# Image indices placed chunk by chunk, image 0's first strips between the chunks, and row sends one turn later, in a fused block-matching and convolution kernel

## The chip, the core and the metric

The kernel runs on one core of a Trainium2 chip. The metric is device time in microseconds (us), the median of several runs of the whole program. The engines are TensorE (PE, matmul; its weight loads are PEld), VectorE (DVE), ScalarE (ACT), GpSimd (POOL) and SyncE (SP). POOL and SP issue nearly all DMAs.

## What is computed

The input is eight images of 32 channels by 128 x 128 in float32. Layer 0 normalises an image in groups of two channels, then finds for each pixel the 8 offsets of a 5 x 5 window whose 3 x 3 patches are nearest, gathers the 8 shifted copies (256 channels), and runs three rounds of a 1 x 1 convolution (256 to 256) and a 3 x 3 depthwise convolution. A grouped 1 x 1 mix of the gathered copies (dct) is multiplied in, two more mixes bring it to 32 channels, and x is added. Layer 1 normalises again, applies one 5 x 5 kernel to each channel and adds.

```python
def _L0_conv_ref(x, dct_w, w1, w2, w3, w4, w5, w6, inv_dct_w, agg_w):
    ...
    xb = _patch_match_stack(x)
    dct = _conv(xb, dct_w, groups=C)
    h = jax.nn.relu(_conv(_conv(xb, w1), w2, groups=CK, pad=1))
    h = jax.nn.relu(_conv(_conv(h, w3), w4, groups=CK, pad=1))
    wiener = jax.nn.sigmoid(_conv(_conv(h, w5), w6, groups=CK, pad=1))
    filt = _conv(wiener * dct, inv_dct_w, groups=C)
    return _conv(filt, agg_w)
...
x = x + _L0_conv_ref(_gn(x), L0_conv_dct_w, L0_conv_w1, L0_conv_w2, L0_conv_w3, L0_conv_w4,
                     L0_conv_w5, L0_conv_w6, L0_conv_inv_dct_w, L0_conv_agg_w)
x = x + _L1_conv_ref(_gn(x), L1_conv_kernel, 1, 2)
```

## The kernel before

**Two streams of work.** The *convolution* of an image is cut into 16 steps of 8 rows, and a 17th step that finishes what lags (`steps`, pairs of image b and step n). The *preparation* of an image makes the offset indices that its gather needs. Image 0 is prepared alone at the start; image b+1 is prepared inside the steps of image b.

**Preparation** (`prep`, L338) works on four row groups of 32 rows, one on each 32 partitions. It loads the image `xn` (one buffer), normalises it, and takes six slices (i) of six rows. In a slice there are six pairs of differences `df` on DVE (L411), their squares on ACT (L419), sums over channels on PE into `pd` (L426), and a copy `sm` that goes to DRAM as `sq` (`squares`). After slices 1, 3, 4 and 5, `costs` is pushed for chunk 0, 1, 2 and 3: eight rows in each row group. It loads `dsum` back, sums the 3 x 3 patches (L475 to L487), turns the result with PE into `pt` and ACT's copy `ct`, and for each row takes four MAX8 and FIND_INDEX8 on DVE (`mx`, `idx`). A counter, `left`, pushes `places` when the last of the 32 rows of maxima is done. `places` (L511) turns offset indices into gather positions: for each of the four row groups, seven DVE operations on `o` and `cn`, two turns on PE (`pi`), two copies on ACT (`li`), two DMAs on POOL into the DRAM table `idxd`. When the four are issued the image is `ready`.

**Gather.** A strip is four rows; it is fetched in two units g. `gather_load` (POOL) loads pixels `xt` (three buffers) once a strip, and two broadcast index tiles `ib` (five buffers). `gather_select` (ACT, L585 and L586) turns them into `sel`, and `gather_pixels` (PE, L600, and a copy `xb` on ACT, L607) picks the pixels. Seven units are loaded and four gathered before the first step; in the loop, pixels run one step ahead and loads three units further.

**A step** of the convolution goes over i = 3, 2, 1, 0: depth i of the three convolutions, each one step behind the one before, and i = 0 for the end of a step (`final_dct`, `final_add`). Depth i has a half on DVE (`depthwise_v`: one ACT and eight DVE operations L689 on the tile `tv`, 10.5 us together) and a half on PE (`depthwise_t`: 48 matmuls `pw`, L709, on the tile `t`). After `pointwise_t`, SP shifts rows inside `t` (L671, L673); `pw` needs them. `rows_before_t` (L617) and `rows_before_v` (L624) send the last rows of `t` and `tv` to their top for the *next* step, on SP; at an image's end a POOL memset stands in for them (L619, L626).

**What sets the order.** PE, DVE and ACT run in program order; the order on POOL and SP is chosen when the program is built. Preparation tasks are generators that wait in four queues: D (DVE work, with a cost in us), A, P and Q (follow-up work on ACT and PE). `tick` is called once in each i and pays out D work: `total / (NS - 2)` us a step, so an image's preparation is spread over 14 steps. `until(cond, 4.0)` instead runs all queues in a loop until a condition holds, with no step in between. Before the first step it runs till image 0 is ready, and at step 15 till the next image is. `prep(b + 1)` is pushed at step 0 of image b.

The order inside one i, which both edits touch, is:

```python
next(new_v, None)            # 8 DVE taps of depth i
if live and i: pointwise_t(i, bi, ni, lws[i - 1], src)
if not i: next(dt, None)     # pw of the depth before
if s < len(steps): unit(gather_pixels, u)
...
if i: next(dt, None)         # pw of the depth before
run("A")
next(dv, None)               # activation, then rows_before_v
next(dt, None)               # activations, then rows_before_t
dv, dt = new_v, new_t
```

Of the kernel before, what the change touches and what calls it, by code (L numbers as in the profile page):

```python
# [43 lines left out]
def bm3d_conv_preact(  # L44
# [293 lines left out]
    def prep(b):  # L338

        xn = load_image(b, nc.gpsimd) if b else first  # L340
        yield "P", 0
        yield "D", 5.5
        st = work.tile([P, 8, 6], F32, name=f"st_{b}", tag="st")
        for i in range(8):
            nc.vector.bn_stats(
                st[:, i], xn[:, 3 + 4 * i : 7 + 4 * i, 2 : 2 + W]
            )
        mv = work.tile([P, 2], F32, name=f"mv_{b}", tag="mv")
        nc.vector.bn_aggr(mv, st.rearrange("p a b -> p (a b)"))
        yield "A", 0  # L350
        nc.scalar.copy(xn[:, :, 0:2], xn[:, :, 2:3].to_broadcast([P, HR, 2]))
        nc.scalar.copy(
            xn[:, :, 2 + W :], xn[:, :, 1 + W : 2 + W].to_broadcast([P, HR, 2])
        )
        mr = yield from group_stats(mv, f"a{b}")
        nc.vector.tensor_scalar(
            xn, xn, mr[:, 0:1], mr[:, 1:2], op0=ALU.subtract, op1=ALU.mult
        )
        push(sources(b, xn))

        idx = work.tile([P, 4, 8, K, 4], U32, name=f"idx_{b}", tag="idx", bufs=1)

        sq = dram.tile([NO // 2, 4, HR - 2, HX], F32, name=f"sq_{b}", tag="sq")
        left = [32]
        for i in range((HR - 2) // SR):
            pd = ps_d.tile([P, SR // 2, HX], F32, name=f"pd_{b}_{i}", tag="pd")

            for aa in ((2, 4), (0, 0), (1, 1), (3, 2), (4, 3), (5, 5)):
                yield "D", PAIR
                push(squares(b, i, pd, xn, aa, sq, idx, left))  # L370

    def sources(b, xn):

# [23 lines left out]
                xt[:, ja:jz, t], xl[:, at : at + 1].to_broadcast([H, jz - ja, C])  # L397
            )

    def squares(b, i, pd, xn, aa, sq, idx, left):  # L400


        r0 = SR * i
        ds = []
        for e in range(2):
            o = 13 + 2 * aa[e] + e
            dy, dx = o // 5 - 2, o % 5 - 2

            ca, cz = max(0, -dx), min(HX, HX - dx)
            df = work.tile([P, SR, HX], F32, name=f"df_{b}_{i}_{o}", tag="df", bufs=4)  # L410
            nc.vector.tensor_sub(  # L411
                df[:, :, ca:cz],
                xn[:, r0 : r0 + SR, ca:cz],
                xn[:, r0 + dy : r0 + dy + SR, ca + dx : cz + dx],
            )
            ds.append((df, ca, cz))
        yield "A", 0
        for df, ca, cz in ds:
            nc.scalar.activation(df[:, :, ca:cz], df[:, :, ca:cz], AF.Square)  # L419
        yield "Q", 0  # L420

        for e in range(2):
            for h in range(2):
                df, ca, cz = ds[e]
                j = 2 * e + h
                nc.tensor.matmul(  # L426
                    pd[C * j : C * (j + 1), :, ca:cz],
                    neg[:, 28 - 4 * aa[e] : 60 - 4 * aa[e]],
                    df[:, SR // 2 * h : SR // 2 * (h + 1), ca:cz],
                    start=aa[0] == 2,  # L430
                    stop=aa[0] == 5,
                    skip_group_check=True,
                )
        if aa[0] < 5:
            return
        sm = work.tile([P, SR // 2, HX], F32, name=f"sm_{b}_{i}", tag="sm", bufs=1)
        nc.scalar.copy(sm, pd)
        for e in range(2):
            for h in range(2):
                j = 2 * e + h  # L440
                nc.gpsimd.dma_start(
                    sq[e::2, :, r0 + SR // 2 * h : r0 + SR // 2 * (h + 1)].rearrange(
                        "o g r x -> o g (r x)"
                    ),
                    sm[C * j : C * j + 24].rearrange("p r x -> p (r x)"),
                )

        q = {1: 0, 3: 1, 4: 2, 5: 3}.get(i)
        if q is not None:
            push(costs(b, q, sq, idx, left))  # L450

    def costs(b, i, sq, idx, left):

        yield "A", 0, 2
        while held:
# [32 lines left out]
        for h in range(0, R, 4):  # L488
# [9 lines left out]
            for q in range(4):  # L498
                yield "D", 1.85
                y = 8 * i + h + q  # L500
                for rg in range(4):
                    c25 = ct[:, q, rg : rg + 4 * NO - 3 : 4]
                    nc.vector.max(mx[:, 4 * q + rg], c25)
                    nc.vector.max_index(
                        idx[:, rg, y // 4, :, y % 4], mx[:, 4 * q + rg], c25
                    )
                left[0] -= 1
                if not left[0]:
                    push(places(b, idx))

    def places(b, idx):  # L511

        dst = idxd[b] = dram.tile([32, K * 4, W], BF16, name=f"idxd_{b}", tag="idxd")
        for rg in range(4):
            yield "D", 2.6
            o = work.tile([P, 256], F32, name=f"o_{b}_{rg}", tag="lin_o", bufs=1)
            ct = work.tile([P, 256], F32, name=f"cn_{b}_{rg}", tag="lin_c", bufs=1)
            nc.vector.tensor_copy(o, idx[:, rg].rearrange("p s k y -> p (s k y)"))
            nc.vector.tensor_scalar(ct, o, 5.0, None, op0=ALU.is_ge)
            for lim in (10.0, 15.0, 20.0):  # L520
                nc.vector.scalar_tensor_tensor(
                    ct, o, lim, ct, op0=ALU.is_ge, op1=ALU.add
                )
            nc.vector.scalar_tensor_tensor(
                o, ct, float(QW - 5), o, op0=ALU.mult, op1=ALU.add
            )
            o3 = o.rearrange("p (s y) -> p s y", y=4)
            nc.vector.tensor_tensor(
                o3,
                o3,  # L530
                cst[:, C_BASE : C_BASE + 4].unsqueeze(1).to_broadcast([P, 64, 4]),
                ALU.add,
            )
            yield "P", 0
            for h in range(2):
                pt = ps_x.tile([P, 512], F32, name=f"pi_{b}_{rg}_{h}", tag="x")
                nc.tensor.transpose(pt[:, :P], o[:, h * P : (h + 1) * P], ident)
                li = work.tile([P, P], BF16, name=f"li_{b}_{rg}_{h}", tag="li")
                nc.scalar.copy(li, pt[:, :P])
                s = 8 * rg + 4 * h  # L540
                nc.gpsimd.dma_start(
                    dst[s : s + 4].rearrange("s k x -> (s k) x"), li
                )
        ready.add(b)

    ready = set()
    xbs, xts, ibs, selss = {}, {}, {}, {}
# [1 line left out]
    def gather_load(b, s4, g):  # L549
# [16 lines left out]
        for k2 in range(2):  # L566
            ib = work.tile(
                [P, 2, 4, W], BF16, name=f"ib_{b}_{s4}_{g}_{k2}", tag="ib", bufs=5
            )
            k0 = 4 * g + 2 * k2  # L570
            nc.gpsimd.dma_start(  # L571
                ib.rearrange("p k y x -> p (k y x)"),
                idxd[b][s4, 4 * k0 : 4 * k0 + 8]
                .rearrange("k x -> (k x)")
                .partition_broadcast(P),
            )
            ibs[b, s4, g, k2] = ib
# [97 lines left out]
    def depthwise_v(i, b, n):  # L675
# [15 lines left out]
                )  # L691
        yield
        nc.scalar.activation(acc, acc, funcs[i - 1])
        rows_before_v(i, b, n)

    def depthwise_t(i, b, n):
# [169 lines left out]

    def unit(stage, u):
        if 0 <= u < len(units) and units[u]:
            stage(*units[u])

    def source(i, b, n):
# [8 lines left out]
    total = 5.5 + 3.3 + 36 * 1.95 + 4 * 4.6 + 32 * 1.85 + 4 * 2.6 + 8 * 2.1  # L880
    owed = [0.0]

    def tick(i):

        now[0] += 1
        owed[0] += total / (NS - 2) * (0.4 if i == 0 else 0.2)
        owed[0] -= run("D", owed[0]) if owed[0] > 0 else 0
        owed[0] = min(owed[0], 6.0)

# [8 lines left out]
    with tc.manual_schedule(engines=ORDERED):  # L898
        push(prep(0))
        push(mixes())  # L900
        until(lambda: 0 in ready, 4.0)
        xbd[0] = dram.tile([P, 2, H, W], F32, name="xbd_0", tag="xbd")
        for i in range(3):
            nc.gpsimd.memset(tb[i][0:64, :, 0], 0.0)
# [3 lines left out]
            unit(gather_pixels, u - 3)  # L908
        u = 4

        dt = dv = iter(())

        later = lambda: None

        for s in range(len(steps) + 2):
            if s < len(steps):
                b, n = steps[s]
                if s == 2:
                    push(bands())
                if n == 0 and b + 1 < NB:  # L920
                    push(prep(b + 1))
                if n == NS - 1 and b + 1 < NB:
                    until(lambda: b + 1 in ready, 4.0)
# [1 line left out]
            for i in (3, 2, 1, 0):  # L925
# [23 lines left out]
                if s < len(steps):  # L949
                    unit(gather_select, u + 1)  # L950
                    unit(gather_load, u + 3)
                    tick(i)
                next(new_v, None)
                if live and i:
                    pointwise_t(i, bi, ni, lws[i - 1], src)
                if not i:
                    next(dt, None)
                if s < len(steps):
# [4 lines left out]
                run("A")  # L963
                next(dv, None)
                next(dt, None)
                dv, dt = new_v, new_t
                if live and not i:
                    later = partial(end, bi, ni, xr, j0, j1)
                if not i and 0 <= s - 1 < len(steps):
                    fins[s - 1] = final_load(*steps[s - 1])  # L970
        later()
        until(lambda: NB - 1 in done, 4.0)

# [61 lines left out]
```

## Time and profile before

| | us |
|---|---|
| Median of 3 runs | 7167.68 (7158.68 to 7188.37) |
| The profiled execution, its own time | 7169.27 |
| Its span, first to last instruction | 7167.5 |
| Mean granted TensorE clock | 0.977 |
| First `pg` (gather) / first `pv` of step 0 of image 0 | 214.4 / 241.6 |
| Step 0 of images 1 and 2 | 1070.0 / 1940.2 |
| Last matmul `pw` begins | 7086.6 |
| PE / DVE / ACT / POOL busy | 6709.5 / 5835.6 / 5061.9 / 2716.4 |

A line of the profile names the engine, the line of the kernel, the operation and the tiles as out<-in. A group's idle figure is the engine's idle time just ahead of its instructions, with what ended it. The slices cut the span in 40 pieces of 179 us; a digit is tenths. The page's chain of what ended last covers only the end of this run, from about 7000 us, so the start and the steps are read from the timeline and from busy times in stretches. Times in those are from the first instruction on.

### The profile page before, as it was taken

The page shows a single profiled execution, that of the slowest core. Times are in us where ns is not written, and L with a number is a line of the kernel's source. Part 1 is how long each engine was busy: PE and PEld are TensorE (multiplying, and loading weights), DVE is VectorE, ACT ScalarE, POOL GpSimd, SP SyncE. Part 2 cuts the span into 40 slices and gives each one's busy share as a digit, 9 for nine tenths or more (in the row PEclk, how much of TensorE's full clock was granted, in tenths as well). Part 3 has the DMA queues.
Part 4 walks back from the last instruction along what each step waited for, and adds up shares of the span by engine and source line. Part 5 has one row for each costly group of instructions (what it writes and reads, how often), then busy time and mean ns, then how long its engine had stood idle before and what let it go on. Part 6 is the DMA issues. An engine that isn't in the chain of part 4 may idle for free. (4 is left out here: it accounts for less than half of the span.)

```text
span 7167.5 us, 229467 instructions
## 1 busy us (share of the span) xinstructions
PE 6709.5 (94%) x100226; PEld 3178.5 (44%) x100226; DVE 5835.6 (81%) x8606; ACT 5061.9 (71%) x6704; POOL 2716.4 (38%) x4599
## 2 busy tenths in 40 slices
PE   4699999999999999999999999999999999999997
PEld 1344444444444444444444444444444444444443
DVE  7689878788788888888888888888888889767675
ACT  4777668677686777767677776877668677676662
POOL 6343335333353333533344333543335333232222
PEclk7799999999999999999999999999999999999999
DMA  3476656667566665756656565666656655556652
GB/s 82 120 163 146 149 136 152 139 148 152 131 157 143 141 152 125 165 147 138 151 125 160 141 149 134 144 156 147 148 134 143 161 137 148 129 148 140 143 136 63
DMA packets 762413, 1007.47 MB, mean 141 GB/s; under 512 B 211425, under 2 KB 575009, under 8 KB 761409
## 3 DMA queue, kind: packets, MB, share of 16 engines
q0 software_dynamic: 375328, 733.44, 42.2%
q1 hardware_dynamic: 381056, 256.86, 17.1%
q8 instruction: 788, 12.91, 0.8%
q10 hardware_dynamic: 5024, 2.49, 0.2%
q14 instruction: 217, 1.77, 0.1%
HBM read 542.24 MB, written 217.01 MB: 106 GB/s over the span
## 5 line engine op out<-in xcount | busy, mean ns | idle before, releaser
L689 DVE SCALAR_TENSOR_TENSOR acc<-tv,dwv,acc 128x1024 f32<-128x1024 f32 (+1 forms) x3264 | 4083.7, 1252 | 214.6 <-ACT acc L686 103.2
L709 PE MATMUL pw<-t,dwd 128*32 128x508 f32 (+6 forms) x19584 | 2174.5, 591 | 151.3 <-DMA t<-t 116.0
L709 PEld LDWEIGHTS pw<-t,dwd 128*32 128x32 f32 (+1 forms) x19584 | 702.9, 111 | 1384.1 <-issue 1182.2
L571 POOL DMA_DIRECT2D ib<-idxd x1024 | 570.9, 558 | 1803.4 <-ACT sel L586 1611.8
L585 ACT ACTIVATE ib<-ib,nplace 128x1024 bf16<-128x1024 bf16 x1024 | 1165.5, 1138 | 16.6 <-DMA ib<-idxd 16.6
L586 ACT ACTIVATE sel<-ib 128x1024 f32<-128x1024 bf16 x1024 | 1084.4, 1059 | 32.6
L661 PE MATMUL p<-acc,lw 128*32 128x256 f32 x17408 | 994.6, 375 | 20.2 <-issue 20.2
L638 PE MATMUL pv<-acc,lw 128*128 128x512 f32 (+1 forms) x2112 | 979.8, 607 | 8.0 <-DVE acc L760 3.9
L607 ACT COPY xb<-pg 128x512 f32<-128x512 f32 x512 | 303.9, 594 | 732.8 <-PE pg L600 732.6
L646 ACT COPY tv<-pv 128x512 f32<-128x512 f32 (+2 forms) x784 | 445.6, 584 | 493.6 <-PE pv L638 483.1
L661 PEld LDWEIGHTS p<-acc,lw 128*32 128x32 f32 x17408 | 565.2, 110 | 441.2 <-issue 99.6
L600 PEld LDWEIGHTS pg<-sel,xt 128*32 128x32 f32 x45056 | 594.8, 111 | 226.2 <-issue 142.7
L721 ACT ACTIVATE acc<-pw 128x512 f32<-128x512 f32 (+1 forms) x816 | 453.3, 585 | 341.1 <-PE pw L709 340.6
L780 DVE TENSOR_TENSOR xr<-xr,pa 128x256 f32<-128x256 f32 (+2 forms) x136 | 55.0, 405 | 765.2 <-PE pa L773 757.3
L600 PE MATMUL pg<-sel,xt 128*32 128x48 f32 x45056 | 598.0, 206 | 84.8 <-issue 69.3
L638 PEld LDWEIGHTS pv<-acc,lw 128*128 128x128 f32 x2112 | 383.9, 193 | 409.8 <-issue 379.2
L411 DVE TENSOR_TENSOR df<-xn 128x786 f32<-128x786 f32 (+2 forms) x576 | 528.7, 967 | 22.1 <-PE pd L426 20.6
L668 ACT COPY t<-p 128x512 f32<-128x512 f32 x800 | 423.8, 571 | 113.3 <-PE p L661 110.1
L686 ACT ACTIVATE acc<-tv,dwv 128x1024 f32<-128x1024 f32 (+1 forms) x408 | 459.8, 1127 | 49.5 <-PE pa L773 32.3
L419 ACT ACTIVATE df<-df 128x786 f32<-128x786 f32 (+2 forms) x576 | 459.6, 862 | 24.5 <-DVE df L411 23.9
L638 PE MATMUL pv<-xb,lw 128*128 128x512 f32 x1024 | 474.8, 606 | 0.0
L757 PE MATMUL pc<-xf,ldct 128*128 128x512 f32 (+2 forms) x1056 | 472.0, 589 | 0.0
(128 smaller groups left out, 6366.3 us busy)
## 6 DMA issues: line engine op xcount, KB each, us to landing
ib<-idxd POOLq DMA_DIRECT2D x1024, 256.0 KB, 4.4
xbd<-xb POOLq DMA_DIRECT2D x128, 1024.0 KB, 8.6
xf<-xbd POOLq DMA_DIRECT2D x480, 256.0 KB, 10.1
t<-t SPq DMA_DIRECT2D x792, 128.0 KB, 4.9
t<-t SPq DMA_DIRECT2D x384, 256.0 KB, 4.9
tv<-tv SPq DMA_DIRECT2D x384, 130.0 KB, 4.0
xt<-xtd POOLq DMA_DIRECT2D x240, 176.0 KB, 5.2
xl<-xs POOLq DMA_DIRECT2D x256, 64.0 KB, 2.5
```

The costliest lines, as they stand in the source:

```text
L411: nc.vector.tensor_sub(df[:, :, ca:cz], xn[:, r0 : r0 + SR, ca:cz], xn[:, r0 + dy : r0 + dy + SR, ca + dx : cz + dx],)
L419: nc.scalar.activation(df[:, :, ca:cz], df[:, :, ca:cz], AF.Square)
L571: nc.gpsimd.dma_start(ib.rearrange("p k y x -> p (k y x)"), idxd[b][s4, 4 * k0 : 4 * k0 + 8] .rearrange("k x -> (k x)") .partition_broadca ...
L585: nc.scalar.activation(ib, ib, AF.Square, bias=nplace)
L586: nc.scalar.activation(sel, ib, AF.Relu, scale=-1.0, bias=1.0)
L600: nc.tensor.matmul(pg[C * j : C * (j + 1), :, xa:xz], xt[:, t], sels[j // 2][:, j % 2, :, xa:xz], start=True, stop=True,)
L638: nc.tensor.matmul(ps[:, :hr], lhsT[:, g, P:CK], src(g)[:, h : h + hr], start=g == 0, stop=g == 1,)
L661: nc.tensor.matmul(ps[C * r : C * (r + 1), e, :nb], lhsT[:, g, s], rows[:, r : r + 4 * nb - 3 : 4], start=g == 0, stop=g == 1,)
L686: nc.scalar.activation(acc, rows, AF.Copy, scale=tap)
L689: nc.vector.scalar_tensor_tensor(acc, rows, tap, acc, op0=ALU.mult, op1=ALU.add)
L709: nc.tensor.matmul(pt[u][C * j : C * (j + 1), :, :nb, xa:xz], dwd[0:hi, i - 1, u, j, dx + 1], t[0:hi, j, :, :nb, xa + dx : xz + dx], start ...
L757: nc.tensor.matmul(ps[:, : z - a], ldct[:, m], xf[:, m, a:z], start=True, stop=True)
```

## The change

First, `places` is called at the end of each `costs`, for that chunk's eight rows in all four row groups, and marks the chunk ready; the table `idxd` is laid out as four groups of eight strips. The loop before the first step no longer waits for the image: `gather_load` of a unit waits (`until`) for the chunk that holds its strip. Strips 0 and 1 need chunk 0, strips 2 and 3 chunk 1, and so on to strips 6 and 7. Since loads run ahead, chunks 0 and 1 fall before the first step, chunk 2 into step 0 and chunk 3 into step 1.

Second, the preparation of image 1 is pushed at step 4 of image 0, not at step 0, and `tick` pays it out over 10 steps instead of 14. The other images keep 0 and 14.

Third, `depthwise_v` yields once more between its activation and `rows_before_v`, and the loop keeps the generator for one more turn (`kept`), so the row send comes after the next depth's `pointwise_t` with its shifts.

```diff
-                left[0] -= 1
-                if not left[0]:
-                    push(places(b, idx))
-    def places(b, idx):
-        dst = idxd[b] = dram.tile([32, K * 4, W], BF16, name=f"idxd_{b}", tag="idxd")
-        for rg in range(4):
-            yield "D", 2.6
...
-            nc.vector.tensor_copy(o, idx[:, rg].rearrange("p s k y -> p (s k y)"))
...
-        ready.add(b)
+        push(places(b, idx, i))
+    def places(b, idx, i):
+        if i == 0:
+            idxd[b] = dram.tile([4, 8, K * 4, W], BF16, name=f"idxd_{b}", tag="idxd")
+        yield "D", 2.6
...
+        nc.vector.tensor_copy(
+            o.rearrange("p (g z) -> p g z", g=4),
+            idx[:, :, 2 * i : 2 * i + 2].rearrange("p g s k y -> p g (s k y)"),
+        )
...
+            nc.gpsimd.dma_start(
+                idxd[b][2 * h : 2 * h + 2, 2 * i : 2 * i + 2].rearrange("g s k x -> g (s k) x"),
+                li,
+            )
+        ready.add((b, i))
+        if i == 3:
+            ready.add(b)
...
         nc.scalar.activation(acc, acc, funcs[i - 1])
+        yield
         rows_before_v(i, b, n)
...
     def unit(stage, u):
         if 0 <= u < len(units) and units[u]:
+            if stage is gather_load:
+                at = (units[u][0], units[u][1] % 8 // 2)
+                until(lambda: at in ready, 4.0)
             stage(*units[u])
...
-        owed[0] += total / (NS - 2) * (0.4 if i == 0 else 0.2)
+        owed[0] += total / (NS - 2 if b else NS - 6) * (0.4 if i == 0 else 0.2)
...
-        until(lambda: 0 in ready, 4.0)
...
-                if n == 0 and b + 1 < NB:
+                if n == (0 if b else 4) and b + 1 < NB:
+                    until(lambda: b in ready, 4.0)
                     push(prep(b + 1))
...
+                next(kept, None)
                 if not i:
                     next(dt, None)
...
-                dv, dt = new_v, new_t
+                kept, dv, dt = dv, new_v, new_t
```

More of the change, by code (lines that the diff above doesn't have):

```diff
@@ L363, in prep @@
         sq = dram.tile([NO // 2, 4, HR - 2, HX], F32, name=f"sq_{b}", tag="sq")
-        left = [32]
         for i in range((HR - 2) // SR):
@@ L369, in prep @@
                 yield "D", PAIR
-                push(squares(b, i, pd, xn, aa, sq, idx, left))
+                push(squares(b, i, pd, xn, aa, sq, idx))
     def sources(b, xn):
@@ L398, in sources, with squares @@
             )
-    def squares(b, i, pd, xn, aa, sq, idx, left):
+    def squares(b, i, pd, xn, aa, sq, idx):
         r0 = SR * i
@@ L449, in squares, with costs @@
         if q is not None:
-            push(costs(b, q, sq, idx, left))
-    def costs(b, i, sq, idx, left):
+            push(costs(b, q, sq, idx))
+    def costs(b, i, sq, idx):
         yield "A", 0, 2
@@ L506, in costs @@
                     )
-                left[0] -= 1
-                if not left[0]:
-                    push(places(b, idx))
-    def places(b, idx):
-        dst = idxd[b] = dram.tile([32, K * 4, W], BF16, name=f"idxd_{b}", tag="idxd")
-        for rg in range(4):
-            yield "D", 2.6
-            o = work.tile([P, 256], F32, name=f"o_{b}_{rg}", tag="lin_o", bufs=1)
-            ct = work.tile([P, 256], F32, name=f"cn_{b}_{rg}", tag="lin_c", bufs=1)
-            nc.vector.tensor_copy(o, idx[:, rg].rearrange("p s k y -> p (s k y)"))
[L519 to L525, printed above, removed]
-            )
[L527 to L543, printed above, removed]
-        ready.add(b)
@@ new lines, in costs @@
+        push(places(b, idx, i))
[3 more added lines that the diff above has]
+        yield "D", 2.6
+        o = work.tile([P, 256], F32, name=f"o_{b}_{i}", tag="lin_o", bufs=1)
+        ct = work.tile([P, 256], F32, name=f"cn_{b}_{i}", tag="lin_c", bufs=1)
+        nc.vector.tensor_copy(
+            o.rearrange("p (g z) -> p g z", g=4),
+            idx[:, :, 2 * i : 2 * i + 2].rearrange("p g s k y -> p g (s k y)"),
+        )
+        nc.vector.tensor_scalar(ct, o, 5.0, None, op0=ALU.is_ge)
+        for lim in (10.0, 15.0, 20.0):
+            nc.vector.scalar_tensor_tensor(ct, o, lim, ct, op0=ALU.is_ge, op1=ALU.add)
+        nc.vector.scalar_tensor_tensor(o, ct, float(QW - 5), o, op0=ALU.mult, op1=ALU.add)
+        o3 = o.rearrange("p (s y) -> p s y", y=4)
+        nc.vector.tensor_tensor(
+            o3,
+            o3,
+            cst[:, C_BASE : C_BASE + 4].unsqueeze(1).to_broadcast([P, 64, 4]),
+            ALU.add,
+        )
+        yield "P", 0
+        for h in range(2):
+            pt = ps_x.tile([P, 512], F32, name=f"pi_{b}_{i}_{h}", tag="x")
+            nc.tensor.transpose(pt[:, :P], o[:, h * P : (h + 1) * P], ident)
+            li = work.tile([P, P], BF16, name=f"li_{b}_{i}_{h}", tag="li")
+            nc.scalar.copy(li, pt[:, :P])
+            nc.gpsimd.dma_start(
+                idxd[b][2 * h : 2 * h + 2, 2 * i : 2 * i + 2].rearrange("g s k x -> g (s k) x"),
+                li,
+            )
+        ready.add((b, i))
+        if i == 3:
+            ready.add(b)
@@ L572, in gather_load @@
                 ib.rearrange("p k y x -> p (k y x)"),
-                idxd[b][s4, 4 * k0 : 4 * k0 + 8]
+                idxd[b][s4 // 8, s4 % 8, 4 * k0 : 4 * k0 + 8]
                 .rearrange("k x -> (k x)")
@@ L881, in bm3d_conv_preact, with tick @@
     owed = [0.0]
-    def tick(i):
+    def tick(b, i):
         now[0] += 1
-        owed[0] += total / (NS - 2) * (0.4 if i == 0 else 0.2)
+        owed[0] += total / (NS - 2 if b else NS - 6) * (0.4 if i == 0 else 0.2)
         owed[0] -= run("D", owed[0]) if owed[0] > 0 else 0
@@ L909, in bm3d_conv_preact @@
         u = 4
-        dt = dv = iter(())
+        dt = dv = kept = iter(())
         later = lambda: None
@@ L951, in bm3d_conv_preact @@
                     unit(gather_load, u + 3)
-                    tick(i)
+                    tick(b, i)
                 next(new_v, None)
@@ L970, in bm3d_conv_preact @@
                     fins[s - 1] = final_load(*steps[s - 1])
+        next(kept, None)
         later()
```

## The prediction

> **What bounds the kernel now.** I read the page's busy shares and slices first, then the timeline of the start, then busy time by step, then the waits.
>
> ```profile
> PE 6709.5 (94%) x100226; PEld 3178.5 (44%) x100226; DVE 5835.6 (81%) x8606; ACT 5061.9 (71%) x6704; POOL 2716.4 (38%) x4599
> ...
> PE   4699999999999999999999999999999999999997
> ...
> PEclk7799999999999999999999999999999999999999
> ```
>
> TensorE (PE) is the bound from the third slice on. In the first two (360 us) it is not, and there its granted clock is low as well. So the start, and a few per cent of PE idleness later, are all there is to win. The timeline of the start, DVE and then PE (start, length, what):
>
> ```profile
> 206.85 0.43 DVE L528 TENSOR_TENSOR o<-o,cst 128x256 f32<-128x256 f32 x1
> ...
> 210.61 0.42 DVE L528 TENSOR_TENSOR o<-o,cst 128x256 f32<-128x256 f32 x1
> ```
> ```profile
> 211.18 0.66 PE L537 MATMUL pi<-cst,o 128*128 128x128 f32 x2 [3.10 <-DVE o L528]
> ...
> 241.55 4.82 PE L638 MATMUL pv<-xb,lw 128*128 128x512 f32 x8
> ...
> 259.15 7.87 PE L709 MATMUL pw<-t,dwd 96*32 96x512 f32 x48 [7.96 <-DMA t<-t]
> ...
> 283.54 3.70 PE L638 MATMUL pv<-xb,lw 128*128 128x512 f32 x8
> ...
> 294.64 5.33 PE L709 MATMUL pw<-t,dwd 96*32 96x512 f32 x48
> ```
>
> The last indices are placed at 211.0. `pv<-xb` marks the steps: step 0 at 241.55, step 1 at 283.54, and by the same kind of row steps 2, 3, 4, 5 and 14 at 336.0, 390.7, 443.9, 493.0 and 946.0. Busy time in stretches cut at such steps (columns: stretch, length, PE, PEld, DVE, ACT, POOL, clock, DMA share, GB/s):
>
> ```profile
> 493.00:946.00 453.00, 431.94 (x6780) 204.81 (x6776) 399.75 (x678) 337.12 (x443) 159.06 (x285) 0.99 0.66 147
> 1117.00:1173.00 56.00, 53.29 (x814) 25.35 (x813) 44.54 (x46) 50.54 (x71) 33.58 (x55) 0.97 0.62 148
> ...
> 2369.00:2427.00 58.00, 52.33 (x776) 23.95 (x772) 54.17 (x81) 40.40 (x54) 22.68 (x40) 0.94 0.63 137
> ...
> 4107.00:4163.00 56.00, 52.06 (x781) 24.66 (x774) 51.90 (x79) 41.22 (x55) 22.67 (x40) 0.97 0.68 144
> ...
> 6712.00:6759.00 47.00, 46.29 (x744) 21.51 (x736) 34.04 (x31) 34.58 (x44) 12.68 (x23) 1.00 0.68 149
> ```
>
> The first is nine steps of image 0 (50.3 us each); the last is a step without preparation: PE 46.3, DVE 34.0. Preparation in a step is added to a PE already full, and DVE has about 13 us to spare. The steps at 2369 and 4107 show what happens when DVE passes 51 us: it is busy 93% and sets the pace.
>
> **Part 1a, places per chunk, and strips between chunks.** No work is added: four groups of seven DVE operations, 2.9 us each (196.86 to 199.75 in the timeline), now follow their own chunk; the tables have the same bytes. What changes is order, so I follow the chain through the changed program's instruction order with the durations of before.
>
> Up to the squares of slice 4 nothing differs: DVE is at 121.9. Places of chunk 0 end at 124.8. ACT has two squares ahead of `li`: 128. POOL issues the index writes, then eight loads of xt (0.49 each), then `ib` at 133, landing after 4.4 (page, part 6): 137. Behind that wait on ACT stand, in order, four `ib`/`sel` pairs (2.2 each) and `xb`, and only then `ct` of chunk 1. DVE, which has work until 133.4, waits for `ct` until 147. Chunk 1 then takes 22.4: eight rows of maxima (1.65 to 1.76 each), four pairs of differences (1.85 each), 1.4 of waiting for the second `ct`. Its places end at 172.6.
>
> ACT has `li` at 174 and two units of selection (4.4 and a copy each) until 184. The load of strip 2 stands on POOL behind `xt` of strip 4, which needs the buffer that PE's last `pg` of strip 1 frees at 185, and behind an image load (0.9): issued 187, landed 192. Three units of selection stand ahead of `ct` of chunk 2: 207. DVE, with sums until 182, idles 25 us. Then 13.2 of maxima and 2.9 of places: 223.1.
>
> On PE `pi` of chunk 2 waits for that, and queued behind it are a `pg` and step 0's `pv`: 225.8 against 241.6. From there the chain is that of before (p, t, 5.7 us of shift, pw at 243.6 for 7.9). DVE has 5.3 of sums, 10.5 of taps, 13.2 of maxima with 6 us of waiting for `ct`, and places until 265.3. `pi` of chunk 3 stands on PE ahead of `p`, so PE waits from 259 to 265. Step 1 starts at 265.4 + 0.7 + 3.6 + 1.1 = 270.8 against 283.5: **-12.7**. Most of the time that chunks 2 and 3 held before comes back as waiting in ACT's order.
>
> Two rules of the Trainium skill bear on these prices. DMA: Bandwidth & Descriptors, "Anatomy of one DMA", puts a Pool-queue DMA at about 2.0 us plus its bytes; a 256 KB `ib` load would be 2.6, an estimate from that page, where the row has 4.4. Three such loads lie on the chain: 5.4 us better by the rule. TensorE: Matmul & The Clock Gate, Part 1, speaks against the change: after an idle window PE restarts at half clock for some 3.4 us, so cutting one idle stretch into several pays that again, 1.7 each. The row says 7.87 against 5.33 for the same 48 matmuls, 2.5 each; two more halts are 3.4 by the rule, 5 by the row. I keep the rows, and one cold start, as before. Bounds: -21 (loads at 2.6, no cold start) and -4 (one more cold start, and one `ib` load at the 10.1 that the equally large `xf` load takes).
>
> **Part 1b, image 1's preparation starts at step 4, not 0.** Steps 1 to 4 lose it. They took 493.0 - 283.5 = 209.5. Three steps without it, 6615 to 6759, take 144, 48 each; with 3 us in step 1, whose shift comes after 4.4 us of selection, 195: **-14.7**. Image 1's ten load issues on POOL now fall among the `ib` loads of steps 0 and 1; they are in the order costed above.
>
> Steps 5 to 13 then carry the rest: 2.9 (normalise) + 36 pairs x 1.85 + 4 x 5.1 (sums) + 32 rows x 1.7 + 4 x 2.9 = 156 us of DVE, 17.3 a step, 51.3 with the 34.0. PE has 50.2: the stretches from 283 to 946 have 51.7 + 51.1 + 49.5 + 48.6 + 431.9 = 632.8 busy, thirteen empty steps would have 601, so with 4 in step 0 the preparation is 36 us of PE, 4.0 a step. If PE bounds, with its present 2.3 of idleness: 52.5 x 9 = 472.5, +19.5 on 453. If DVE bounds at the 0.939 of the five fullest steps I found (0.91 to 0.96): 54.6 x 9 = 492, +39. The steps are mixed (the first three mostly differences, which load PE too, the later ones maxima, which don't), so the middle: **+29**.
>
> **Part 1c, images 1 to 6.** Their preparation keeps its rate, but places leave step 13 and spread: the DVE load of preparation at steps 10, 12, 13 goes from 10.5, 16.0, 13.7 to 14.5, 13.7, 12.4. PE idles some 17 us an image in steps 8 to 13. A small smoothing, -1.5 an image: **-9**, between -24 and +12.
>
> **Part 2, rows sent later.** The waits (in total, times, longest), and one shift on SP:
>
> ```profile
> PE pw L709 <- DMA t<-t: 116.0, 63, 8.0
> ```
> ```profile
> SPq L671 <- ACT xb L607: 2692.2, 306, 18.4
> SPq L617 <- PE pw L709: 1292.0, 261, 18.0
> SPq L624 <- DVE acc L689: 1093.5, 290, 14.1
> ```
> ```profile
> 1618.18 0.59 SPq L671 DMA_DIRECT2D t<-t  x1
> 1618.82 0.61 SPq L673 DMA_DIRECT2D t<-t  x1
> 1620.95 0.50 SPq L624 DMA_DIRECT2D tv<-tv  x1
> ```
>
> PE does wait for shifts, 116 us. But SP waits for ACT before most shifts L671: it stands idle and issues as `t` ends, so the row send L624 holds none of them up; here it already follows. And SP's list in the changed program differs only by 33 swaps of L624 with the neighbouring L617, and one L624 two places earlier in the first steps. L617 and L624 both serve the next step, some 40 us on. **0**; if that cover were gone, 34 x 0.5 = 17 us late, and a gain of 5 is my other bound. The Pool memsets at an image's end move one turn, and nobody waits for them.
>
> **Sum.** -12.7 - 14.7 + 29 - 9 = -7 on the profiled execution's 7169.3: 7162 (the median shown is 1.6 lower).
>
> **Rivals.**
> *Faster*: PE stays the bound. Heavy steps +19.5, the start near its good end (-20), images 1 to 6 at theirs (-24): -20 - 14.7 + 19.5 - 24 = -39, 7130. For it: the step at 1117 carries 16 differences with PE at 53.3 of 56 and DVE at 44.5. Against: that is one step, with slack behind it.
> *Slower*: DVE becomes the bound in steps 5 to 13 of image 0. Nine full steps in a row leave nothing to absorb its waits in order for `pc` and `pa` (757 us for `pa` over the run). At a share of 0.87, 59 a step: +78 - 27 - 9 = +42, 7211. The sign turns at 0.94, half a per cent is passed below 0.88. Against: the lowest of the five has 0.91.
> *The second edit does what it says*: all 116 us of shift waits gone, 7053. SP's order speaks against it.
>
> **How the numbers follow.** Half a per cent, 36 us, is about what a measurement of this kernel can tell from no change. Likeliest 0.60 (7140 to 7185 by itself), faster 0.26, slower 0.12, second edit 0.02; 0.02 of the faster case stays within half a per cent. So faster 0.26, same 0.62, slower 0.12. The range goes down to 7112, the faster case with 2 us less of PE idleness in each heavy step, and up to 7206, the slower one at 0.876.
>
> **What would show it.** Step 0 near 226 and step 1 near 271; DVE gaps near 133 and 182; PE waiting for `o` twice after 200. Step 5 some 27 us earlier than 493 and that lead gone by step 14; DVE at 51 in steps 5 to 13, busy 0.93 to 0.96. Shift waits still about 116. Wrong if step 14 is early by over 20 or late by over 20, or if image 1, step 0 to step 0 (1070.0 to 1940.2 before), differs by over 5.

## The result, and the profile after

The changed kernel takes 7133.63 us (median of 8 runs, 7121.63 to 7151.16) against 7166.93 for the kernel before in 8 runs beside it: ratio 0.9954, 95% interval 0.9937 to 0.9970, some 33 us faster. A second set, taken with the experiments, gave 0.9957 (0.9944 to 0.9969). The forecast, "within half a per cent", holds by a little (0.46%, and the interval goes up to 0.63%), 7133.63 lies in the range, and the single number, 7162, is 28 us too high. The two profiled executions differ by 7167.5 - 7129.4 = 38.1 us of span.

The page after:

```profile
PE 6700.9 (94%) x100226; PEld 3166.8 (44%) x100226; DVE 5840.1 (82%) x8606; ACT 5061.7 (71%) x6706; POOL 2738.3 (38%) x4599
...
PE   4699999999999999999999999999999999999997
...
PEclk8899999999999999999999999999999999999999
```

Little in it tells the two kernels apart beside the clock of the first two slices. Again the start and the steps have to be read by themselves. The start on DVE and on PE (start, length, what, idle before and what ended it):

```profile
147.34 0.21 DVE L502 MAX8 mx<-ct 128x8 f32<-128x25 f32 x1 [13.42 <-ACT ct L495]
...
206.86 0.20 DVE L502 MAX8 mx<-ct 128x8 f32<-128x25 f32 x1 [27.38 <-ACT ct L495]
```
```profile
223.22 0.66 PE L534 MATMUL pi<-cst,o 128*128 128x128 f32 x2 [22.60 <-DVE o L525]
...
225.68 4.62 PE L637 MATMUL pv<-xb,lw 128*128 128x512 f32 x8
...
247.81 7.11 PE L709 MATMUL pw<-t,dwd 96*32 96x512 f32 x48 [12.13 <-DMA t<-t]
...
268.70 0.66 PE L534 MATMUL pi<-cst,o 128*128 128x128 f32 x2 [6.53 <-DVE o L525]
269.29 4.94 PE L660 MATMUL p<-acc,lw 128*32 128x256 f32 x64
...
275.07 3.70 PE L637 MATMUL pv<-xb,lw 128*128 128x512 f32 x8
...
291.44 7.03 PE L709 MATMUL pw<-t,dwd 96*32 96x512 f32 x48 [3.01 <-DMA t<-t]
```

DVE waits twice for `ct` behind ACT's selections, as forecast, and PE stands twice at `pi`. Step 0 begins at 225.7 (before 241.6), step 1 at 275.1 (283.5). By `pv<-xb` the later starts, after minus before, are: step 5 -27.5, step 14 -0.1, step 0 of image 1 **+6.8**, then -4.2, -8.3, -16.3, -28.8, -39.2, -35.6 at images 2 to 7. So image 0 ends behind, and the whole gain is made in images 1 to 6. In stretches (columns: stretch, length, PE, PEld, DVE, ACT, POOL, clock, DMA share, GB/s), steps 5 to 13 of image 0 and then images 1 to 6, after; and images 1 to 6 before:

```profile
465.50:946.00 480.50, 453.54 (x6949) 213.69 (x6945) 439.39 (x762) 368.98 (x489) 214.66 (x357) 0.98 0.67 151
1076.80:6228.20 5151.40, 4972.99 (x75159) 2359.04 (x75155) 4368.96 (x6424) 3788.20 (x5021) 2040.56 (x3424) 0.99 0.62 146
```
```profile
1070.00:6263.70 5193.70, 4983.84 (x75158) 2369.62 (x75154) 4366.27 (x6426) 3792.01 (x5021) 2022.06 (x3424) 0.99 0.62 145
```

Length less PE's busy time is what PE stood idle in images 1 to 6: 209.9 us before, 178.4 after. These 31.5 are the greater part of the 42.3 by which the stretch is shorter. The other 10.8 are PE busy time for the same matmuls. In the fourteen traces of this document that time lies between 4968 and 4997, and it goes with the granted clock of the execution: 4968 in the one at 0.980, 4997 in the one at 0.973. How much of it is the change's, one trace can't say (the last section comes back to it). So I judge the runs below by PE's idle time, beside their times.

The waits after, PE's for shifts and SP's own, which answer to those shown of before:

```profile
PE pw L709 <- DMA t<-t: 109.4, 53, 12.1
```
```profile
SPq L670 <- ACT xb L606: 2979.8, 317, 209.8
SPq L616 <- PE pw L709: 1278.7, 259, 15.1
SPq L623 <- DVE acc L688: 1105.1, 290, 19.4
```

SP waits for the engines as before (the 209.8 is SP's wait from the start to the first shift, at 237.35), and PE's waits for shifts are 109.4 against 116.0.

### The profile page after: what moved, and what is told of

Same layout as the page of the kernel before. It is cut to its first block, busy times and chain, and to the rows that moved or that the text cites. A ratio compares the mean times of both kernels' runs of the same rounds, so it can differ in the third digit from the quotient of the medians.

```text
span 7129.4 us, 229485 instructions
## 1 busy us (share of the span) xinstructions
PE 6700.9 (94%) x100226; PEld 3166.8 (44%) x100226; DVE 5840.1 (82%) x8606; ACT 5061.7 (71%) x6706; POOL 2738.3 (38%) x4599
## 5 line engine op out<-in xcount | busy, mean ns | idle before, releaser
L688 DVE SCALAR_TENSOR_TENSOR acc<-tv,dwv,acc 128x1024 f32<-128x1024 f32 (+1 forms) x3264 | 4084.0, 1253 | 223.1 <-ACT acc L685 109.5
L709 PE MATMUL pw<-t,dwd 128*32 128x508 f32 (+6 forms) x19584 | 2179.5, 592 | 156.8 <-DMA t<-t 109.4
L660 PE MATMUL p<-acc,lw 128*32 128x256 f32 x17408 | 994.1, 375 | 10.3 <-issue 10.0
L599 PEld LDWEIGHTS pg<-sel,xt 128*32 128x32 f32 x45056 | 591.2, 111 | 225.7 <-issue 126.1
L410 DVE TENSOR_TENSOR df<-xn 128x786 f32<-128x786 f32 (+2 forms) x576 | 529.0, 969 | 17.2 <-PE pd L425 14.6
```

The source lines that it names most:

```text
L410: nc.vector.tensor_sub(df[:, :, ca:cz], xn[:, r0 : r0 + SR, ca:cz], xn[:, r0 + dy : r0 + dy + SR, ca + dx : cz + dx],)
L599: nc.tensor.matmul(pg[C * j : C * (j + 1), :, xa:xz], xt[:, t], sels[j // 2][:, j % 2, :, xa:xz], start=True, stop=True,)
L660: nc.tensor.matmul(ps[C * r : C * (r + 1), e, :nb], lhsT[:, g, s], rows[:, r : r + 4 * nb - 3 : 4], start=g == 0, stop=g == 1,)
L688: nc.vector.scalar_tensor_tensor(acc, rows, tap, acc, op0=ALU.mult, op1=ALU.add)
L709: nc.tensor.matmul(pt[u][C * j : C * (j + 1), :, :nb, xa:xz], dwd[0:hi, i - 1, u, j, dx + 1], t[0:hi, j, :, :nb, xa + dx : xz + dx], start ...
```

## Experiments

Twelve runs, each timed against the kernel before on the same chip. The theory after the result was A: the gain comes from where the places of images 1 to 6 now stand. Its rival B: it comes from the row sends. C and D are about image 0's full steps, E and F about why A. The table sums up; "idle" is PE's in images 1 to 6 of the profiled execution, "step 8" its mean in step 8 of those images, "pi" PE's wait there for `o`, and "image 1" the start of its step 0, after minus before. Idle times and starts are from one trace each. The kernel before had other medians beside the experiments than in the first row, so compare by the ratio: 7161.12 beside rows only, no rows, places only and step 2; 7161.85 beside changed again, image 0 only, step 1 and pause 2.6; 7155.37 beside the last four.

| kernel | median us (runs) | ratio to before, 95% interval | idle | step 8 | pi | image 1 |
|---|---|---|---|---|---|---|
| before | 7166.93 (8) | 1 | 209.9 | 3.9 | 16.3 | 0 |
| changed | 7133.63 (8) | 0.9954, 0.9937 to 0.9970 | 178.4 | 0.4 | 3.9 | +6.8 |
| changed, again | 7134.99 (14) | 0.9957, 0.9944 to 0.9969 | 177.2 | 0.5 | 2.2 | +12.2 |
| rows only | 7164.66 (14) | 1.0006, 0.9990 to 1.0021 | 215.6 | 3.7 | 16.1 | +5.4 |
| changed, no rows | 7143.85 (22) | 0.9974, 0.9965 to 0.9983 | 175.8 | 0.4 | 2.6 | +18.1 |
| places only | 7134.82 (15) | 0.9968, 0.9955 to 0.9980 | 171.8 | 0.4 | 3.8 | +13.7 |
| image 0 only | 7177.29 (22) | 1.0028, 1.0019 to 1.0038 | 196.9 | 3.8 | 19.3 | +15.7 |
| prep from step 2 | 7116.90 (6) | 0.9942, 0.9921 to 0.9964 | 174.3 | 0.4 | 1.4 | -3.7 |
| prep from step 1 | 7127.95 (14) | 0.9962, 0.9945 to 0.9979 | 171.5 | 0.5 | 2.2 | +5.2 |
| pause 2.6 | 7127.16 (7) | 0.9954, 0.9933 to 0.9975 | 165.5 | 0.6 | 0.6 | +7.7 |
| pause 0.9 | 7115.36 (6) | 0.9941, 0.9922 to 0.9961 | 176.5 | 2.1 | 0 | -6.5 |
| pause after chunk 1 | 7152.64 (22) | 0.9994, 0.9981 to 1.0006 | 191.1 | 3.9 | 3.3 | +19.7 |
| start, step 2, pause | 7132.11 (22) | 0.9969, 0.9958 to 0.9980 | 185.2 | 0.5 | 1.4 | +15.6 |
| the same, no rows | 7136.85 (12) | 0.9972, 0.9958 to 0.9985 | 168.7 | 0.5 | 0.5 | +9.7 |

**Rows only.** The second edit on the kernel before.

```diff
         nc.scalar.activation(acc, acc, funcs[i - 1])
+        yield
         rows_before_v(i, b, n)
...
                     pointwise_t(i, bi, ni, lws[i - 1], src)
+                next(kept, None)
...
-                dv, dt = new_v, new_t
+                kept, dv, dt = dv, new_v, new_t
```

> The kernel before with the second edit alone: the row send tv<-tv one turn later, nothing else changed. Theory A (the gain of 33 us comes from the order of DVE work in the preparation of images 1 to 6): no change, 7160 to 7174 us, the interval of the ratio holds 1, and the waits of pw for t stay at 114 to 118 us. Theory B (the gain comes from the row sends, because shifts get through SP earlier): 7125 to 7140 us, ratio about 0.995, image 1 from step 0 to step 0 about 7 us shorter than 870.1.

No change in time, idle 215.6, waits for shifts 122.1 (a little above what A said). B falls.

**Changed, no rows.** The same lines taken out of the changed kernel.

> The changed kernel without the second edit: places per chunk and image 0's strips between chunks stay, the row send is back where it was. Theory A: the gain stays, 7126 to 7142 us (ratio to the kernel before 0.994 to 0.997). Theory B: the gain is gone or turned, 7165 to 7180 us, image 1 from step 0 to step 0 back at about 870.

Idle in images 1 to 6 is as low as with the edit (175.8), the time is 7143.85, just above the band of A. What is missing against the changed kernel is, as far as one trace each tells, in image 0 (image 1 begins at +18.1, against +6.8 and +12.2).

**Places only.** Places per chunk; image 0's start, its rate and the rows as before.

```diff
-                left[0] -= 1
-                if not left[0]:
-                    push(places(b, idx))
...
+        push(places(b, idx, i))
```

> Places per chunk for all images, but the loop before the first step waits for the whole of image 0 again, image 1 is prepared over 14 steps from step 0, and the row send is where it was. Theory A: images 1 to 6 get 7 us shorter each as in the changed kernel, image 0 as before: -42 us, 7120 to 7132 us, step 0 of image 1 between 1066 and 1072. Since image 1's preparation in image 0's steps is spread in the same way, image 0 may gain some 5 us too. Theory B: 7155 to 7172 us.

```profile
1083.70:6245.10 5161.40, 4989.57 (x75159) 2367.93 (x75155) 4364.45 (x6417) 3789.47 (x5019) 2046.34 (x3423) 0.99 0.62 146
```

Idle is 5161.4 - 4989.6 = 171.8: the full gain in images 1 to 6 without image 0's new start and without the row edit. Image 0 did not gain the 5 us I thought possible; image 1 begins 13.7 late. So A stands on its mechanism, while the time, 7134.82, is above A's 7120 to 7132.

**Image 0 only.** The other half: images 1 to 7 make their places at the end again.

```diff
-        push(places(b, idx, i))
+        for c in (i,) if b == 0 else range(4) if i == 3 else ():
+            push(places(b, idx, c))
```

> Image 0 as in the changed kernel (places per chunk, strips between chunks, image 1 prepared in steps 4 to 13), but images 1 to 7 make their places at the end as before, and the row send is where it was. My prediction for this part alone: -12.7 - 14.7 + 29 = +2 us. Theory A (images 1 to 6 give the whole gain): PE idle in images 1 to 6 at 205 to 216 us, step 0 of image 1 between 1074 and 1090, 7165 to 7178 us. If the better start gave the gain after all: 7130 to 7150 us.

```profile
1085.70:6254.20 5168.50, 4971.61 (x75159) 2365.64 (x75155) 4365.41 (x6422) 3792.10 (x5021) 2044.36 (x3423) 0.99 0.62 146
```
```profile
PE pi L535 <- DVE o L526: 19.3, 6, 3.2
```

Idle is 196.9, more than half of it back (A said 205 to 216; this trace is of the fastest of the 22 runs), the wait of `pi` is 19.3 again, and the time is 0.28% *longer* than before: image 0's new start with the crowded steps 4 to 13 behind it is a loss by itself.

**Prep from step 2, and from step 1.** The changed kernel with image 1's preparation pushed earlier and paid over 12 or 13 steps.

```diff
-        owed[0] += total / (NS - 2 if b else NS - 6) * (0.4 if i == 0 else 0.2)
+        owed[0] += total / (NS - 2 if b else NS - 4) * (0.4 if i == 0 else 0.2)
...
-                if n == (0 if b else 4) and b + 1 < NB:
+                if n == (0 if b else 2) and b + 1 < NB:
```

> The changed kernel, with image 1's preparation pushed at step 2 of image 0 and paid over 12 steps, not at step 4 over 10. Theory C (the heavy steps 4 to 13 of image 0 lose the 32 us lead because DVE, at some 51 us a step, leaves no room for its waits; at 47 us it does): lead at step 2 as in the changed kernel, about 15 us, and steps 2 to 13 at 51 each, so step 0 of image 1 comes 8 to 15 us earlier than in the changed kernel (1062 to 1069) and the time is 7118 to 7127 us. Theory D (the cost of a preparation is the same wherever it is put, as PE has to do it anyway): step 0 of image 1 at 1073 to 1081, the time 7130 to 7138 us.

> The changed kernel, with image 1's preparation pushed at step 1 of image 0 and paid over 13 steps, not at step 4 over 10. Theory C (DVE at 51 us a step leaves no room for its waits; the thinner the preparation is spread the less PE idles in image 0): step 0 of image 1 at 1058 to 1066, PE idle in image 0 at 45 to 51 us (60.8 in the changed kernel, 51.2 with the push at step 2), 7112 to 7122 us. Theory D (the cost is the same wherever it is put): 1066 to 1077, idle 51 to 61, 7118 to 7138 us; the wait for chunk 3 at the start of step 1 can also cost 3 to 6 us, which goes to D's side.

From step 2: image 1 begins at 1066.3, PE's idle time in image 0 falls from 60.8 to 51.2, and the median is 7116.90, a microsecond below C's band. From step 1: image 1 at 1075.2, idle 57.4. That is D's side. Thinner is not steadily better; in these traces 12 steps fall better than 10 or 13, though the intervals of the three ratios overlap. The next runs show the same kind of thing.

**Pause 2.6.** The kernel before with one line more, which pays for nothing.

```diff
                 if not left[0]:
                     push(places(b, idx))
+        if i == 0 and b:
+            yield "D", 2.6
```

> The kernel before, with one line more: after the sums and maxima of chunk 0 of images 1 to 7 the D queue pays out 2.6 us for nothing, where the changed kernel pays for chunk 0's places. No work is moved; all D work behind it falls 2.6 us of payment later, so that step 8 has 4 differences instead of 6 and step 9 has 6 instead of 4. Theory E (phase: PE loses time in step 8 since DVE has one pair of differences too many there): PE idle in step 8 falls from 3.9 to about 0.4 us an image, in images 1 to 6 from 210 to some 185 us, the wait of pi for o stays near 16 us, 7138 to 7150 us. Theory F (what counts is that the places leave the end of the preparation, where PE stands at pi and waits for o): step 8 stays at 3.5 to 4, the sum of images 1 to 6 at 205 to 215, 7155 to 7168 us.

```profile
1077.70:6211.60 5133.90, 4968.44 (x75158) 2357.72 (x75154) 4366.37 (x6426) 3790.53 (x5021) 2023.08 (x3424) 0.99 0.62 147
4080.50:4129.50 49.00, 48.40 (x766) 23.38 (x765) 43.67 (x73) 41.02 (x54) 20.28 (x35) 1.00 0.53 136
```
```profile
PE pi L539 <- DVE o L530: 0.6, 2, 0.4
```

This is the run that decides. All places are still made at the end, nothing is moved between chunks, and yet idle falls to 165.5 and the ratio, 0.9954, is that of the whole change. F falls. E's step 8 came (3.9 to 0.6), but the gain is larger than E said (idle 185, 7138 to 7150), and the wait of `pi` goes as well (16.3 to 0.6), which I had tied to where the places are. The same step of the same image, step 8 of image 4, before:

```profile
4107.40:4162.70 55.30, 51.36 (x777) 24.38 (x773) 51.20 (x79) 40.63 (x54) 22.67 (x40) 0.97 0.68 144
```

Before, DVE's 51.2 us are as much as PE's 51.4, and the step takes 55.3. With the pause DVE has 43.7, PE idles 0.6, and the step takes 49.0. Of the 6.3 us, 3.3 are idle time saved. The other 3.0 are PE busy time: 766 matmuls for 777, at a granted clock of 1.00 for 0.97.

**Pause 0.9, and pause after chunk 1.** Two that should move only part of it.

```diff
-            yield "D", 2.6
+            yield "D", 0.9
```
```diff
-        if i == 0 and b:
+        if i == 1 and b:
```

> The kernel before with a pause of 0.9 us instead of 2.6 after chunk 0. By the order of DVE's instructions this takes one pair of differences out of step 8 (4 instead of 6 operations) as the longer pause does, but puts it together with the sums into step 9, leaves step 12 as it was (six rows of maxima and sums), and moves the last places to step 14. Theory E, step by step: step 8 idle at 0.4 to 0.8 us (before 3.9), step 12 at 3.5 to 4 as before (with the longer pause 1.8), step 9 at 2 to 4 (before 1.6): images 1 to 6 at 180 to 200 us, 7138 to 7152 us. If any delay helps as much as the longer one (for instance because the last places leave the full step 13): 160 to 172 us and 7122 to 7135 us.

> The kernel before with the 2.6 us pause after chunk 1 instead of chunk 0: steps 1 to 9 keep their order, steps 10 to 14 get the shift. Theory E: step 8 stays at 3.5 to 4 us of PE idle (with the pause after chunk 0: 0.6), step 12 falls to about 2, the wait of pi for o falls from 16 to under 5; images 1 to 6 at 180 to 198 us, 7140 to 7155 us. If step 8 is not the cause but only shows it, the sum falls as far as with the earlier pause, to 160 to 172.

The later pause behaves as E said: step 8 keeps its 3.9 us, the wait of `pi` falls to 3.3, idle to 191.1. Image 0 begins image 1 19.7 late, so the time stays at 7152.64. The short pause goes against my step-by-step forecast: step 8 falls only to 2.1, step 12 to 1.7 instead of staying, idle is 176.5, between what I gave E and its rival, and the median, 7115.36, is below both. What I had not seen is that step 12's idle time before is mostly the one halt at `pi` (3.2 us in five of the six images), which any delay removes. Counted by steps, over the six images: the short pause saves 10 us in step 8, 12 in step 12 and 5 each in steps 10 and 13, of 33 in all; the later pause saves nothing in step 8, 10 in step 10 and 7 in step 12, of 19; the pause of 2.6 after chunk 0 saves 20 in step 8, 11 in step 12 and only 3 in step 10, of 44.

**Start, step 2 and pause together**, with and without the row edit: meant to beat everything.

> The version that the runs so far point to: image 0 with places per chunk and its strips between them, image 1 prepared from step 2 over 12 steps, images 1 to 7 with their places at the end and the 2.6 us pause after chunk 0, row sends one turn later. Theory E (phase): PE idle in images 1 to 6 at 160 to 172 us as with the pause alone (165.5), step 0 of image 1 near 1066: 7102 to 7116 us, faster than the changed kernel by 20 to 30 us. If the two gains don't add up: 7120 to 7130 us.

> The same as the version with everything (image 0's start, preparation from step 2, pause), but with the row send where it was before. The second edit gave +4 us on the kernel before and -9 on the changed one, both about as large as their uncertainty. If it is worth nothing: within 6 us of the version with it. If it helps where image 0's steps are full: 6 to 12 us slower, all of it between step 0 of image 0 and step 0 of image 1.

It does not: 7132.11 and 7136.85. Image 1 begins 15.6 and 9.7 late, where without the pause it was 3.7 early. PE idles 8.0 and 10.0 us in step 10 of image 0, and 8.8 and 11.6 in step 12, where "prep from step 2" had 3.6 and 2.6. What suits a 14-step payment spoils the 12-step one; whether it is the pause or the places of image 1, which stand at the end again in these two, was not taken apart. In images 1 to 6 both pay out DVE's work as "pause 2.6" does, and their idle time is 185.2, 168.7 and 165.5. The first has the row edit besides, and rows only had 6 us more idle time than before; but the changed kernel had 178.4 and 177.2 with it and 175.8 without, so such a difference is more likely the scatter of single executions.

The best two, "prep from step 2" and "pause 0.9" (six runs each), are 0.6% faster than before. Their intervals overlap the changed kernel's, so neither is shown to beat it.

## Why the prediction was right or wrong

*Part 1a, the start.* The working held to the end of chunk 2: DVE's gap of 13.42 us at 133.9 (worked out 13.6), places of chunk 1 ending at 172.1 (172.6), the second gap 27.4 (25), `pi` at 223.2 (223.1), step 0 at 225.7 (225.8). Step 1 came at 275.1, not 270.8. The term that failed is the shift, put at 5.7 us: `pw` began at 247.8 and not 243.6. The second shift was issued from 238.07 to 238.70 and `pw` began 9.1 us later; before, it was issued from 254.15 to 254.78, and `pw` began 4.4 later. Between 230 and 262 us five `ib` loads and two of `xn` (image 1) were issued, and the Pool queue's packets took 51% of the DMA engines' time (before, between 245 and 275, 39%, with six `ib` loads and none of `xn`). I had costed these loads on POOL and not on the DMA engines that the shift needs. That they are what held the shift is read from this coincidence; no run moves them away. The 4.2 us run on to the places of chunk 3 (268.6 for 265.3), and PE restarts cold once more: 4.94 us for the `p` that takes 3.66 elsewhere. The gain at step 1 is -8.5, inside the bounds.

The two rules weighed there: the `ib` loads that ended ACT's two waits took 3.8 us (134.06 to 137.82) and 6.4 us (186.16 to 192.61) from issue to use. The row's 4.4 lies between; the 2.6 estimated from the Trainium skill, DMA: Bandwidth & Descriptors, "Anatomy of one DMA", is too short for both. For a restart, the groups after halts took 1.3, 1.8 and 1.7 us more than their like (4.94, 7.11 and 7.03 against 3.66 and 5.33), at a granted clock of 0.73, 0.75 and 0.76 where the like group at 283.1 has 1.00. That is nearer the 1.7 that I had estimated from the Trainium skill, TensorE: Matmul & The Clock Gate, Part 1, than the row's 2.5. And there was the further cold start that I left out of the sum.

*Part 1b, image 1's preparation later.* Steps 1 to 4 took 190.4 us, -19.1 (forecast -14.7; its own terms, 195 - 209.5, make -14.5), so step 5 was at -27.5 as forecast. Steps 5 to 13 took 480.5, +27.5 (forecast +29), PE busy 94% of them and DVE 91%, 48.8 a step. PE stayed the bound, and the slower rival fell. Two things were missed. The preparation did not end by step 13: step 14 took 50.5 us for 43.6, which makes the +6.8. And the +27.5 is one value of a wide scatter: the same steps cost +33.2, +38.5 and +39.5 in the other three traces with the same start and ten-step payment (changed again, changed without rows, image 0 only). That the first trace met the forecast so closely is luck. Image 0 as a whole costs +7 to +18, not the +2 of the sum.

*Part 1c, images 1 to 6: this is the step that failed.* "A small smoothing, -1.5 an image: -9", with bounds of -24 to +12. Measured in idle time: -31.5, or 5.3 an image, beyond the bound. Image 1 took 859.1 us for 870.2, which by the 5 us I had named is a sign of being wrong. Six traces with places per chunk have 172 to 178, three with places at the end and no pause 197 to 216. I looked at the steps to which or from which places move (10, 12, 13). DVE's preparation there came about as forecast (in its program order 10.3, 14.6 and 13.8 us before, 14.4, 12.6 and 12.3 after), but these steps gave more than the 9: over the six images PE's idle time in step 10 fell from 25 to 12 us and in step 12 from 22 to 14, while step 13 kept 13 to 14. And everything behind the new places in the D queue shifts too. In step 8 two differences leave and the seven operations of chunk 0's places come; the sums of chunk 1 go from step 9 to step 10. I did not count steps 8 and 9, though I had shown step 8, at 4107, as one where DVE sets the pace. I also priced nothing for PE's halt at `pi`, which stands in step 12 and which the waits of before list:

```profile
PE pi L537 <- DVE o L528: 16.3, 6, 3.2
```

Step 8 gives (3.9 - 0.4) x 6 = 21 us, step 10 gives 13, step 12 gives 8 (12 of `pi`, less new waits) and step 15 gives 5; steps 2, 9 and 11 take back 16. That a shift of the queue is enough, with no places moved, is shown for step 8 and `pi` by the 2.6 us pause after chunk 0, and for step 10 and most of `pi` by the one after chunk 1. The changed kernel has a payment of 2.6 us, that of the places, at both points; no run has both pauses. One rival is not tested: the order on POOL and SP is chosen anew for every program, so each of these kernels may differ there too.

What exactly holds PE in step 8 is only partly settled. The amount of preparation doesn't explain it: in that step of DVE's program it is 11.2 us in the changed kernel and 10.3 before. But before, DVE comes into the step late. Of its taps (1.3 us each, 24 to a step), 20.8 fall between PE's starts of steps 7 and 8 and 28.8 between those of steps 8 and 9, in the mean of the six images; after the change it is 23.7 and 22.5. And the loads of `dsum` fall there too, on top of a shift. DMA transfers in the 13 us around that shift, step 8 of image 4, before and after (copies, KB each, median us to landing):

```profile
t<-t SPq DMA_DIRECT2D x2, 128.0 KB, 6.0
dsum<-sq POOLq DMA_DIRECT2D x1, 240.0 KB, 7.0
dsum<-sq POOLq DMA_DIRECT2D x8, 20.0 KB, 3.6
```
```profile
t<-t SPq DMA_DIRECT2D x2, 128.0 KB, 2.4
```

The 0.9 us pause tells part of it. Before, PE halts in each of the six images about 20 us into the step, 7 us in all, on the matmuls that need this shift. With that pause the first load of `dsum` is issued 15.0 us into the step (image 4), where it was 10.8, behind the shift at 11.2; the early halt is gone in all six images, and of the 16 us of later halts 12.6 are left. With the 2.6 us pause 3 us are left. So about 7 of the 23 us go with the loads on the shift. What holds PE later in the step stays open.

*Part 2, rows later: 0.* On the kernel before +4 us, on the changed one -9 (the two intervals just meet), on the last pair -5, less than its interval. Nothing steady, and the shift waits don't go with the edit: 89 to 125 us in six traces with it, 88 to 116 in eight without. Held.

*Sum.* By the two traces: -8.5 - 19.1 + 27.5 + 6.9 to the start of image 1, -42.3 in images 1 to 6, -2.6 after. Forecast: -12.7 - 14.7 + 29 - 9. The mechanism of the faster rival, PE bound and images 1 to 6 at their good end, is what came, only by another road: 1c alone gives its gain, and image 0 none. That 7133.63 lies in the range is owed to the range's width: the term that made the gain was put at -9.

## What to carry to other kernels

When background work is paid out in slices beside a loop, any edit to it shifts all that stands behind it in the queue; list what each step holds before and after, and look first at the steps where a second engine has as much to do as the bound one, and at every halt of the bound engine that the waits list. Before crediting a rearrangement with a gain of half a per cent, try a delay of the same size that does nothing, at each point where the rearrangement pays for something. A gain won by such a shift is real, but it belongs to the alignment: it need not add to another, and the next edit can lose it.

## What was not expected of the hardware

The granted clock, averaged over the span, differs between executions of one and the same kernel, and the time with it: in 44 executions of the kernel before, those at 0.974 took 7178 us (mean of 4), at 0.977 7155 (14), at 0.979 7143 (1), about 7 us for each 0.001, and 0.001 of the span is 7 us. That is most of the scatter of single runs here, and why one trace's length says less than its idle time.

The traces show where the clock falls. In all fourteen, between 360 and 6900 us, it is either whole or half. It falls to half for 3.4 us or a small multiple, 26 to 46 times in a trace. Of these 490 falls, 489 have a halt of PE of 1 us or more in the 5 us before them (8% of instants taken at random have one). But not every halt is followed by a fall: within 3.5 us of its end, 10% are of the halts of 1 to 2 us, 65% of those of 2 to 3, 82% of those of 3 to 4, and all 67 longer ones. So some halts cost more than their own length, as the slow groups of part 1a did. Which of the short ones are followed by a fall, no run shows.

Kernels differ in it too. The mean clock was 0.9777 in 14 runs of the changed kernel and 0.9760 in 44 of the kernel before on the same chip, which at 7 us for 0.001 makes 12 us (an estimate) of the 24.5 between their mean times; "image 0 only" had 0.9757 beside the same 44. That fits the fewer halts in images 1 to 6, but no run sets the clock apart from the halts.
